# A four-layer graph network on one core: the small matmuls grouped into three visits a group, one pool of eight PSUM banks, and the first layer's coefficients planned one step earlier

## The chip, the cores and the metric

The kernel runs on one core of one Trainium2 chip. The metric is device time in microseconds (us) for one execution of the whole program. A core has five engines that take their instructions in order, each from its own stream: TensorE (PE in the profile; its weight loads are listed apart as PEld), VectorE (DVE), ScalarE (ACT), GpSimd (POOL) and SyncE (SP), which here issues the DMA transfers. TensorE writes its results to PSUM, which this kernel cuts into eight banks of 128 partitions by 512 floats.

## The reference, cut to what matters

The input is `x`, 128 graphs of 64 nodes with 512 features each (fp32), a 64 by 64 adjacency matrix for each graph, and a node mask of ones. Four layers follow each other, each inside a residual connection and a layer norm:

```python
# layer 0
s = (x @ w) @ a
A = tanh((s_i + s_j) / 8) * 8;  A = where(A >= 0, A, 0.1 * A)
A = exp(A) * adj;  A = A / A.sum(-1);  A = A * adj.sum(-1)
out0 = A @ x @ w
# layer 1
weight = adj * exp(q @ k.T);  out1 = (weight / weight.sum(-1)) @ v
# layer 2
agg = adj @ (k * mask);  w = mask * sum(q * agg, -1) / sqrt(512)
out2 = softmax(w over the nodes) * v
# layer 3 (hypergraph convolution, twice: 512 -> 1024 -> 512)
h = layer_norm(relu(Dn * (H @ (Be * (H.T @ (x @ W1)))) + b1))
out3 = Dn * (H @ (Be * (H.T @ (h @ W2)))) + b2 + x
# each layer
x = layer_norm(x + out)
```

`q`, `k` and `v` are products of `x` with 512 by 512 weights, and `H` is the pattern of the nonzero entries of `adj`.

## The kernel before, in words

**Tiling.** Two graphs make one tile of 128 tokens, two tiles make a group of 256 tokens, and there are 32 groups. The four layers of one group are written out in `run(g)` (line 962) as 16 steps. What depends on the adjacency alone is made for two groups at a time in `prepare_chunk` (line 656), so the work repeats with a period of two groups.

**How the order comes about.** Nothing is issued while `run(g)` is executed. Every instruction, or small bundle of instructions, is recorded as an `Op` (line 55) with its engine, an estimated cost, the buffers it reads and writes, and a key. The key of an operation of group g starts at `BASE[g]` plus its place among the 16 steps; the starts of neighbouring groups are 4 apart, so about four groups are under way at once, each in another layer. `keys_by_what_follows` (line 101) moves each key according to the length of the work that still depends on the operation, and keeps the lead that it was given (`urgent`). `Order.run` (line 118) then plays through a schedule: for each engine it keeps a heap of operations whose inputs are there, and takes the one with the lowest key for which all needed buffers are free. It then emits them in the order found, and the engine wrapper `pinned` (line 1127) fixes that order. All instructions pass through one line of this wrapper, so every row of the profile says L1133, and the rows are told apart by the names of the tiles they write and read.

**TensorE's forms.** The planner knows four modes of a PE operation. "whole" uses the 128 by 128 array at once. "quarters" divides it into four 64 by 64 arrays, and "columns" into two of 128 by 64. "any" can be done in either way: `over_graph` (line 926), which sums a column over the nodes of a graph, is one 128-row matmul in the whole array or two 64-row ones in quarters. The program counts in matmuls; the profile shows about two records for each (21227 for 10870).

- The large products with weights run whole. `seven_products` (line 806) does a block product with seven multiplications of half-size blocks in place of eight. Two running sums stay in a pair of PSUM banks (names `chx` and `chz` in the profile) and two more products take a single bank each (`bank`).
- `gathered` (line 764) multiplies tokens by a 64 by 64 matrix for each graph, as 16 small matmuls for each tile, in quarters. It is called four times for each group: once in layer 0 (`bank<-e,x`), once with `gm` in layer 3 on `x` and twice on the hidden `h` (`bank<-kept,h`). An ACT copy takes the result out of PSUM.
- `scores` (line 910) runs in columns, 8 matmuls for each tile (`bank<-k,k`), in layers 1 and 2.
- `emit_po` (line 1025) applies layer 1's weights to `v`: four matmuls of 512 columns in quarters (`bank<-k,e`).
- `emit_g` in `prepare_chunk` prepares the adjacency in quarters (`bank<-kept,kept`, `bank<-ones,adj`, `bank<-w,kept`).

A stretch of PE work between leaving the whole array and coming back to it is called a visit to the divided array below. In `Order.run`, a PE operation in the mode that the array is in may be preferred to one with a lower key, if its key is at most `NEAR` (0.5, while whole) or `FAR` (6.0, while divided) higher. A change of mode is charged with 145 or 60 ns (`TURN`, `TURN_DIVIDED`).

**PSUM.** Four banks are of the kind "bank", and two pairs of the kind "pair" take the other four (lines 284 to 286). If an operation cannot start because buffers are lacking, all kinds that it needs are put on hold for later operations of that engine in that search (`held.update(need)`).

**Layer 0's coefficients** are lines 971 to 993: for each tile a row product with `u0_b` on DVE and a scaled diagonal on ACT, then `over_graph` on PE, tanh on ACT, a DVE step, exp on ACT, a DVE product with the adjacency, `over_graph` again, a reciprocal and a last product on DVE. Then `gathered` of step 1 uses them.

**Transfers.** SP streams the weights from DRAM into eight buffers (`ring`, `streamed`, line 622). It may run ahead of the lowest unfinished step by `AHEAD` (3.5). The token tiles are loaded by `load_x` (line 359), whose key lies 6 ahead of the group's start.

Of the kernel before, what the change touches and what calls it, by code (L numbers as in the profile page):

```python
# [54 lines left out]
class Op:  # L55
    __slots__ = ("engine", "cost", "emit", "key", "missing", "users", "takes", "touches", "start", "bytes", "step", "mode", "port", "behind", "group", "args")


class Order:
# [4 lines left out]

    NEAR, FAR = 0.5, 6.0
    AHEAD = 3.5

    def __init__(self, slots):
        self.slots = {kind: list(range(n))[::-1] for kind, n in slots.items()}
        self.ops, self.key, self.group = [], 0.0, None  # L70

    def add(self, engine, cost, reads, writes, emit, urgent=0.0, size=0, mode=None, port=False):
        o = Op()
        o.engine, o.cost, o.emit, o.key, o.step = engine, cost, emit, self.key - urgent, self.key
        o.start, o.mode, o.port, o.behind, o.group, o.args = None, mode, port, None, self.group, ()
        o.users, o.takes, o.touches, o.bytes = [], [], [], size
        before, bufs = set(), []
        for tokens, write in ((reads, False), (writes, True)):
            for b in tokens:
                b, cells = b if isinstance(b, tuple) else (b, range(b.cells))  # L80
                if b not in bufs:
                    bufs.append(b)
                for c in cells:
                    if c in b.writer:
                        before.add(b.writer[c])
                    if write:
                        before.update(b.readers[c])
                        b.writer[c], b.readers[c] = o, []
                    else:
                        b.readers[c].append(o)  # L90
        before.discard(o)
        o.missing = len(before)
        for p in before:
            p.users.append(o)
        for b in bufs:
            b.left += 1
            if b.kind is not None:
                o.touches.append(b)
        self.ops.append(o)

    def keys_by_what_follows(self):
# [8 lines left out]
        for o in reversed(self.ops):  # L110
            if o.group is not None:
# [4 lines left out]
                o.key = o.step - urgent  # L116

    def run(self):

        ready = {e: [] for e in self.LATENCY}  # L120
        free_at = {e: 0 for e in self.LATENCY}
        number = {o: i for i, o in enumerate(self.ops)}
        events, n, link, mode = [], 0, 0, None
        port_free, port_user, landed = 0, None, []
# [5 lines left out]
        while len(done) < len(self.ops):  # L130
# [4 lines left out]
            for e, heap in ready.items():  # L135
                while free_at[e] <= now:
                    skipped, held, found = [], set(), None
                    while heap:
                        if e == "SP" and heap[0][0] > far or found and heap[0][0] > found[0] + (self.NEAR if mode == "whole" else self.FAR):
                            break  # L140
                        item = heappop(heap)
                        need = defaultdict(int)
                        wants = [b for b in item[2].touches if b.slot is None]
                        for b in wants:
                            need[b.kind] += 1
                        if item[2].port and port_free > now:
                            skipped.append(item)
                        elif all(k not in held and len(self.slots[k]) >= c for k, c in need.items()):
                            fits = e != "PE" or item[2].mode in (mode, "any")
                            if found is None or fits:  # L150
                                if found:
                                    skipped.append(found)
                                found, takes = item, wants
                            else:
                                skipped.append(item)
                            if fits or found[0] < 0:
                                break
                        else:
                            held.update(need)
                            skipped.append(item)  # L160
                    for item in skipped:
                        heappush(heap, item)
# [4 lines left out]
                    if e == "PE":  # L167
                        if found.mode == "any":
                            found.mode = "whole" if mode in ("whole", None) else "quarters"
                            found.args = (found.mode == "whole",)  # L170
                        if found.mode != mode:
                            turn = self.TURN if "whole" in (found.mode, mode) else self.TURN_DIVIDED
                        mode = found.mode
                    found.start = now
                    done.append(found)
# [59 lines left out]
def kernel(  # L235
# [47 lines left out]
    kind("col", 40, 16)  # L283
    kind("bank", 4, D, space=psum)
    pairs = [[psum.tile([P, D], FP, name=f"{c}{i}") for c in ("chx", "chz")] for i in range(2)]
    kinds["pair"] = pairs

# [7 lines left out]

    def pe(cost, reads, writes, emit, urgent=0.0, mode="whole"):
        order.add("PE", cost, reads, writes, emit, urgent, mode=mode)

    def dve(n, reads, writes, emit, urgent=0.0, port=None):

        if port is None:
            port = all((b[0] if isinstance(b, tuple) else b).kind not in ("bank", "pair") for b in reads)
        order.add("DVE", w_dve(n), reads, writes, emit, urgent, port=port)
# [352 lines left out]
    def prepare_chunk(c):  # L656
# [31 lines left out]

        pe(720, [turned, hA, bh, w], [*ps, gm], emit_g, mode="quarters")
        for t in range(2):  # L690
# [73 lines left out]
    def gathered(tokens, view, right, reads):  # L764
# [13 lines left out]
        for t in range(GT):  # L778
            pe(470, [tokens(t), *reads], [ps[0][t], ps[1][t]], lambda t=t: emit(t), mode="quarters")
        for h in range(2):  # L780
# [25 lines left out]
    def seven_products(a, s, pieces, first, more, across=False):  # L806


        pieces = iter(pieces)
        pair = Buf("pair", 2)  # L810

        def times(ps, left, start=True):
            piece, view = next(pieces)
            bank = (lambda: pair.t[ps]) if isinstance(ps, int) else (lambda: ps.t)
            token = pair[ps] if isinstance(ps, int) else ps
# [3 lines left out]
            def emit():  # L819
                l, b, o = left[1](), view(), bank()  # L820
                if across:
# [9 lines left out]

            pe(w_pe(P, 2 * chunks) if across else w_pe(width, chunks), [left[0], piece], [token], emit)
            return token, lambda: bank()[:, :width]

# [27 lines left out]
    def scaled_into(at, f, own, n, base=None):  # L862


        def add(k, token, ps, base):
            dst = at[k]
            t = own.start + int(k[0]) - 1
            dve(n + 40, [token, f, base[0]], [dst[0]], lambda: nc.vector.scalar_tensor_tensor(
                dst[1](), ps(), f.t[:, t : t + 1], base[1](), ALU.mult, ALU.add), NOW)
# [4 lines left out]
    def plain_into(b):  # L874

        at = block_views(b, lambda: b.t.rearrange("p (t d) -> p t d", t=GT))
        return (lambda k, token, ps: act(D // 2, [token], [at[k][0]], lambda: nc.scalar.copy(at[k][1](), ps()), NOW),
                lambda k, token, ps: dve(D // 2, [token, at[k][0]], [at[k][0]],
                                         lambda: nc.vector.tensor_add(at[k][1](), ps(), at[k][1]()), NOW))
# [30 lines left out]
    def scores(xT, zT):  # L910

        ps = Buf("bank", GT)
        for t in range(GT):
# [8 lines left out]

            pe(480, [xT[xT_cells(t)], zT[xT_cells(t)]], [ps[t]], emit, mode="columns")
        return ps

    def over_graph(v, ps):
# [5 lines left out]

        pe(w_pe(P), [v], [ps], emit, mode="any")

    def z_into(zT, bias=None):
# [11 lines left out]
        def first(k, token, ps):  # L947
            if bias is None:
                act(2 * P, [token], [cell(k)], lambda: nc.scalar.copy(at(k), two(ps)), NOW)
            else:  # L950
                for c in range(2):
                    col = 2 * (int(k[1]) - 1) + c
                    act(P + 100, [token, bias], [cell(k)], lambda c=c, col=col: nc.scalar.activation(
                        at(k)[:, c], two(ps)[:, c], AF.Identity, bias=bias.t[:, col : col + 1]), NOW)

        def more(k, token, ps):
            dve(2 * P, [token, cell(k)], [cell(k)], lambda: nc.vector.tensor_add(at(k), two(ps), at(k)), NOW)

# [3 lines left out]
    def run(g):  # L962
# [10 lines left out]


        s = Buf("col", GT)
        diag, e, ps_s = Buf("e", GT), Buf("e", GT), Buf("bank")
# [15 lines left out]
        dve(7 * GT * N, [ps_e], [rs], lambda: nc.vector.reciprocal(flat(rs.t), ps_e.t[:, : GT * N]), NOW)  # L992
        dve(GT * N, [e, rs], [e], lambda: nc.vector.tensor_mul(e.t, e.t, rs.t))
        step(1)
        left = left_side(gathered(*of_x, lambda h, t: e.t[halves[h][0], t, :], [e]))
# [34 lines left out]

        pe(w_pe(D), [e1, v], po, emit_po, mode="quarters")
        for t in range(GT):
# [171 lines left out]
```

## Time and profile before

The execution that was profiled is one of the four runs.

| | us |
|---|---|
| runs | 2172.2, 2174.02, 2174.33, 2179.66 |
| median | 2174.17 |
| the profiled execution, its own time | 2172.2 |
| its span, first to last instruction | 2170.3 |
| PE busy within the span | 2143.8 |
| DVE / ACT / POOL busy | 1534.9 / 854.6 / 384.2 |

The time of an execution is 1.9 us longer than the span. In a wait, the name behind the arrow is what released the engine; "issue" stands where the profile shows nothing that the engine waited for.

The stream of instructions itself is fetched by its own DMA queue (q8 in the table of queues), in 168 packets and 2.75 MB, that is 16 KB a packet. PE and PEld together have 42454 records, and 168 packets to those come to about 256 instructions a packet.

### The profile page before, as it was taken

How to read it: one execution, taken by the hardware profiler on the slowest of the kernel's cores; microseconds unless marked ns; L12 is line 12 of the kernel's file. 1: busy time of each engine (PE TensorE's matmuls, PEld its weight loads, DVE VectorE, ACT ScalarE, POOL GpSimd, SP SyncE). 2: the span in 40 equal slices, each digit the busy share in tenths (PEclk: the TensorE clock that was granted, in tenths of full speed). 3: DMA queues.
4: the chain of work that ended last, by engine and by line, in shares of the span. 5: the costliest groups of instructions: out<-in, count | busy, mean ns of one | idle time of the engine just before them, and what ended most of it. 6: DMA issues, size and time to landing. Idle time of an engine off the chain costs nothing.

```text
span 2170.3 us, 52324 instructions
## 1 busy us (share of the span) xinstructions
PE 2143.8 (99%) x21227; PEld 1727.3 (80%) x21227; DVE 1534.9 (71%) x3967; ACT 854.6 (39%) x1812; POOL 384.2 (18%) x399
## 2 busy tenths in 40 slices
PE   8999999999999999999999999999999999999998
PEld 4897787777888878888878888778888788888866
DVE  5787767677776767767676776767767777666675
ACT  2444343343443433443434443434434334333433
POOL 1112211021120212112122111211202221112111
PEclk9999999999999999999999999999999999999999
DMA  9865667656656666666576556666566666566476
GB/s 302 292 216 209 214 212 272 232 198 229 218 196 222 202 229 216 228 205 212 199 237 227 210 195 219 221 234 219 192 216 206 232 222 212 196 211 216 152 254 207
DMA packets 174304, 476.39 MB, mean 220 GB/s; under 512 B 35760, under 2 KB 45296, under 8 KB 174064
## 3 DMA queue, kind: packets, MB, share of 16 engines
q1 hardware_dynamic: 174064, 473.05, 64.0%
q8 instruction: 168, 2.75, 0.5%
q14 instruction: 72, 0.59, 0.1%
HBM read 443.33 MB, written 29.66 MB: 218 GB/s over the span
## 4 chain that ended last, share of the span: by engine, by line
PE 98%; DMA 1%; ACT 0%; issue 0%; DVE 0%; SPq 0%; DVEq 0%; ACTq 0%
PE bank L1133 40%; PE chx L1133 35%; PE chz L1133 23%; DMA ring<-w 0%; ACT k L1133 0%; DMA k<-in_wk_dram 0%; DMA ring<-3b 0%; ACT x L1133 0%; DVE col L1133 0%; DVE x L1133 0%; ACT u_b L1133 0%; ACT bw_b L1133 0%; SPq L1133 0%; DVEq L1133 0%; ACTq L1133 0%
## 5 line engine op out<-in xcount | busy, mean ns | idle before, releaser
L1133 PE MATMUL chx<-ring,k 128*128 128x256 f32 (+1 forms) x1664 | 477.2, 417 | 1.4 <-ACT k L1133 1.2
L1133 PE MATMUL bank<-ring,k 128*128 128x256 f32 (+1 forms) x1536 | 420.5, 416 | 0.3 <-ACT k L1133 0.3
L1133 PEld LDWEIGHTS chx<-ring,k 128*128 128x128 f32 x1664 | 309.0, 190 | 94.9 <-issue 56.2
L1133 POOL TENSOR_TENSOR col<-col,mhalf 128x2 f32<-128x2 f32 (+1 forms) x161 | 111.4, 692 | 1416.2 <-DVE col L1133 578.9
L1133 PEld LDWEIGHTS bank<-ring,k 128*128 128x128 f32 x1536 | 284.7, 190 | 82.9 <-issue 51.1
L1133 ACT COPY k<-bank 128x512 f32<-128x512 f32 (+1 forms) x448 | 228.1, 559 | 227.4 <-PE bank L1133 200.4
L1133 ACT ACTIVATE x<-x,col,col 128x512 f32<-128x512 f32 x256 | 195.4, 808 | 237.6 <-DVE col L1133 237.2
L1133 PE MATMUL chz<-ring,h 128*128 128x256 f32 (+1 forms) x768 | 242.8, 452 | 0.0
L1133 DVE SCALAR_TENSOR_TENSOR x<-chx,col,x 128x256 f32<-128x256 f32 x384 | 173.9, 478 | 73.0 <-PE chx L1133 70.8
L1133 PEld LDWEIGHTS chx<-k,m 128*128 128x128 f32 x1536 | 191.1, 192 | 26.1 <-issue 24.3
L1133 PE MATMUL chx<-k,m 128*128 128x128 f32 x1536 | 203.9, 276 | 0.0
L1133 PE MATMUL chz<-ring,k 128*128 128x256 f32 x768 | 200.4, 386 | 0.0
L1133 DVE SCALAR_TENSOR_TENSOR x<-bank,col,x 128x256 f32<-128x256 f32 (+1 forms) x256 | 137.5, 548 | 81.5 <-PE bank L1133 78.1
L1133 PEld LDWEIGHTS chz<-ring,h 128*128 128x128 f32 x768 | 142.6, 190 | 49.6 <-issue 34.9
L1133 PE MATMUL chx<-ring,h 128*128 128x256 f32 (+1 forms) x640 | 181.4, 422 | 0.1
L1133 DVE BATCH_NORM_STATS2 col<-x 128x6 f32<-128x512 f32 x256 | 174.8, 688 | 7.2
L1133 PEld LDWEIGHTS chz<-ring,k 128*128 128x128 f32 x768 | 140.8, 191 | 21.4 <-issue 2.4
L1133 PEld LDWEIGHTS chx<-ring,h 128*128 128x128 f32 x640 | 120.4, 190 | 35.3 <-issue 18.9
L1133 DVE SCALAR_TENSOR_TENSOR x<-chz,col,x 128x256 f32<-128x256 f32 x192 | 92.3, 481 | 76.4 <-PE chz L1133 75.8
L1133 PEld LDWEIGHTS chz<-k,m 128*128 128x128 f32 x1024 | 127.2, 192 | 12.8 <-issue 12.4
L1133 ACT ACTIVATE h<-h 128x512 f32<-128x512 f32 x128 | 80.7, 632 | 140.7 <-DVE h L1133 140.3
L1133 PE MATMUL chz<-k,m 128*128 128x128 f32 x1024 | 135.2, 275 | 0.0
(120 smaller groups left out, 2795.9 us busy)
## 6 DMA issues: line engine op xcount, KB each, us to landing
ring<-3a SPq DMA_DIRECT2D x224, 512.0 KB, 4.5
ring<-3b SPq DMA_DIRECT2D x224, 512.0 KB, 4.3
ring<-v SPq DMA_DIRECT2D x189, 512.0 KB, 4.4
ring<-w SPq DMA_DIRECT2D x93, 512.0 KB, 4.4
x<-in_x_dram SPq DMA_DIRECT2D x32, 512.0 KB, 4.9
ring<-v SPq DMA_DIRECT2D x63, 256.0 KB, 3.5
out_dram<-x SPq DMA_DIRECT2D x31, 512.0 KB, 4.6
ring<-w SPq DMA_DIRECT2D x31, 256.0 KB, 5.0
```

Source lines behind the costliest of these rows:

```text
L1133: made = f(*args, **kwargs)
```

## The change

Four things change.

1. **The choice of the next PE operation.** It moves to a function `choose`, which sees all operations that could start. While the array is whole, it turns to divided work only if that work's lowest key is below the lowest whole key by more than `NEAR` (now 0.8), or by more than 0 if at least `ENOUGH` (48) small matmuls are waiting. While it is divided, it goes on with divided work that is within `FAR` (now 4.0) of the lowest whole key, the same mode first, up to `BURST` (84) matmuls in one visit. Each divided operation now carries its number of matmuls. An operation of mode "any" is taken when it has the lowest key, in the mode the array is in.
2. **PSUM.** The two pairs and the four banks become one pool of eight banks. `seven_products` takes two of them as its pair, and a token of a new kind `product`, of which there are three, limits how many block products are under way.
3. **Holding back.** An operation that cannot start puts only those kinds on hold that it lacks.
4. **Layer 0's coefficients** get keys that are one step lower (`EARLY`), from the row product to the last product.

```diff
-    NEAR, FAR = 0.5, 6.0
+    NEAR, FAR = 0.8, 4.0
+    ENOUGH = 48
+    EARLY = 1.0
+    BURST = 84
     AHEAD = 3.5
...
-        o.engine, o.cost, o.emit, o.key, o.step = engine, cost, emit, self.key - urgent, self.key
+        o.engine, o.cost, o.emit, o.key, o.step = engine, cost, emit, self.key - urgent - self.early, self.key
...
+    def choose(self, found, mode, burst):
+
+        whole, either = found.get("whole", []), found.get("any", [])
+        divided = sorted(found.get("quarters", []) + found.get("columns", []), key=lambda f: f[0][:2])
+        first = min((f[0] for f in (whole, divided, either) if f), key=lambda f: f[0][:2])
+        if first[0][0] < 0 or first[0][2].mode == "any" or not (whole and divided):
+            return first
+        if mode == "whole":
+            ahead = whole[0][0][0] - divided[0][0][0]
+            enough = sum(f[0][2].matmuls for f in divided) >= self.ENOUGH
+            return divided[0] if ahead > (0 if enough else self.NEAR) else whole[0]
+        fits = [f for f in divided if burst + f[0][2].matmuls <= self.BURST and f[0][0] <= whole[0][0][0] + self.FAR]
+        if not fits:
+            return whole[0]
+        same = [f for f in fits if f[0][2].mode == mode]
+        return (same or fits)[0]
...
-                        if e == "SP" and heap[0][0] > far or found and heap[0][0] > found[0] + (self.NEAR if mode == "whole" else self.FAR):
+                        if e == "SP" and heap[0][0] > far:
                             break
...
-                            fits = e != "PE" or item[2].mode in (mode, "any")
-                            if found is None or fits:
-                                if found:
-                                    skipped.append(found)
+                            if e == "PE":
+                                skipped.append(item)
+                                found_pe.setdefault(item[2].mode, []).append((item, wants))
+                                if item[0] < 0:
+                                    break
+                            else:
                                 found, takes = item, wants
-                            else:
-                                skipped.append(item)
-                            if fits or found[0] < 0:
                                 break
                         else:
-                            held.update(need)
+                            held.update(k for k, c in need.items() if k in held or len(self.slots[k]) < c)
                             skipped.append(item)
+                    if found_pe:
+                        found, takes = self.choose(found_pe, mode, burst)
+                        skipped.remove(found)
...
+                        burst = 0 if mode == "whole" else burst + found.matmuls
...
-    kind("bank", 4, D, space=psum)
-    pairs = [[psum.tile([P, D], FP, name=f"{c}{i}") for c in ("chx", "chz")] for i in range(2)]
-    kinds["pair"] = pairs
+    kind("bank", 8, D, space=psum)
+    kinds["product"] = [None] * 3
...
-        pe(720, [turned, hA, bh, w], [*ps, gm], emit_g, mode="quarters")
+        pe(720, [turned, hA, bh, w], [*ps, gm], emit_g, mode="quarters", matmuls=40)
...
+        going, pair = Buf("product"), [Buf("bank") for _ in range(2)]
         pieces = iter(pieces)
-        pair = Buf("pair", 2)
...
-            pe(w_pe(P, 2 * chunks) if across else w_pe(width, chunks), [left[0], piece], [token], emit)
-            return token, lambda: bank()[:, :width]
+            pe(w_pe(P, 2 * chunks) if across else w_pe(width, chunks), [left[0], piece, going], [token], emit)
+            return (token, going), lambda: token.t[:, :width]
...
+        order.early = order.EARLY
         s = Buf("col", GT)
         diag, e, ps_s = Buf("e", GT), Buf("e", GT), Buf("bank")
...
         dve(GT * N, [e, rs], [e], lambda: nc.vector.tensor_mul(e.t, e.t, rs.t))
+        order.early = 0.0
         step(1)
```

`gathered` gets `matmuls=16`, `scores` 8, `over_graph` 2 and `emit_po` 4, and the readers of a product's result take its token pair. No instruction's arithmetic, shape or count on DVE, ACT, POOL or SP is edited; the number of PE matmuls depends on the mode in which the planner finds the array at each `over_graph`.

## The prediction

> **What bounds the kernel now.** I read the page's share of each engine first, then its chain of waits.
>
> ```profile
> span 2170.3 us, 52324 instructions
> PE 2143.8 (99%) x21227; PEld 1727.3 (80%) x21227; DVE 1534.9 (71%) x3967; ACT 854.6 (39%) x1812; POOL 384.2 (18%) x399
> PEclk9999999999999999999999999999999999999999
> PE 98%; DMA 1%; ACT 0%; issue 0%; DVE 0%; SPq 0%; DVEq 0%; ACTq 0%
> ```
>
> PE is busy for 99% of the span, at full clock in every slice, and it is 98% of the chain. So a gain can only come from fewer or cheaper turns inside PE's stream, or from the few waits that PE has. The PE waits of the whole run are the next view: what was waited for, total us, times, longest.
>
> ```profile
> PE bank L1133 <- issue: 6.4, 6, 3.4
> PE bank L1133 <- DMA k<-in_wk_dram: 6.1, 1, 6.1
> PE bank L1133 <- DVE e L1133: 3.4, 2, 2.2
> PE bank L1133 <- ACT k L1133: 1.5, 3, 0.7
> PE chx L1133 <- ACT k L1133: 1.2, 1, 1.2
> PE bank L1133 <- ACT u_b L1133: 0.7, 1, 0.7
> ```
>
> The wait for the first weights (6.1) is not touched. Of the others about 13 us are within reach. What a visit to the divided array costs is hidden in "busy"; the timeline of PE shows it (start, us, records):
>
> ```profile
> 1006.43 1.06 PE L1133 MATMUL chx<-k,m 128*128 128x128 f32 x8
> 1007.42 1.15 PE L1133 MATMUL bank<-k,k 128*64 128x64 f32 x32
> 1008.50 0.33 PE L1133 MATMUL bank<-e,same 64*64 64x128 f32 x2
> ...
> 1009.44 0.41 PE L1133 MATMUL bank<-e,same 64*64 64x128 f32 x4
> 1009.78 1.13 PE L1133 MATMUL chx<-ring,k 128*128 128x256 f32 x4
> 1010.75 1.05 PE L1133 MATMUL bank<-k,m 128*128 128x128 f32 x8
> ```
>
> I go by starts, since records overlap. Within a mode a 128x256 record takes 216 ns, a 128x128 one 112, a pair of 128x64 59, four 64x64 ones 58. From 1006.43 to 1007.42 eight records of 112 (0.90) take 0.99: +0.09 for the entry. The first divided bundle is +0.05 late, the last takes +0.09 longer, and the first whole product behind it takes 0.97 instead of 0.86: +0.10. Together a visit costs 0.335 us, and a turn from columns to quarters within it about 0.148.
>
> Two stretches of two groups each, the kernel's period (us; PE, PEld, DVE, ACT, POOL busy; clock, DMA share, GB/s), show a steady state in which PE has no gap except in one of them:
>
> ```profile
> 1007.42:1139.35 131.93, 131.67 (x1326) 106.96 (x1325) 93.54 (x245) 52.43 (x111) 23.18 (x24) 1.00 0.64 215
> 1139.35:1270.75 131.40, 131.40 (x1326) 106.84 (x1325) 93.55 (x245) 52.34 (x111) 23.17 (x24) 1.00 0.64 216
> ```
>
> **The change part by part.**
>
> *Turns.* Counted in the two programs' instruction order, the visits go from 118 to 107 (seven per two groups become six), and turns within a visit from 56 to 61. So 11 x 0.335 = -3.7 and 5 x 0.148 = +0.7. `over_graph` now mostly runs whole: 74 calls change from two 64-row matmuls (0.212 us) to one of 128 rows (0.223), +0.8. Sum **-2.2**. This is small next to the words "three visits a group": before already has 3.5.
>
> *Fetch of instructions.* The waits put down to "issue" are these (PE timeline, one place):
>
> ```profile
> 428.26 1.16 PE L1133 MATMUL bank<-e,x 64*64 64x64 f32 x64
> 429.24 0.87 PE L1133 MATMUL bank<-kept,h 64*64 64x64 f32 x44
> 433.49 0.51 PE L1133 MATMUL bank<-kept,h 64*64 64x64 f32 x18 [3.38 <-issue]
> ```
>
> PE stops in the middle of a bundle whose inputs it has. Counting PE and PEld records along the run, eight such stops (240, 341, 430, 766, 1029, 1293, 1556 and 1885 us) lie at the same place modulo 256, and the instruction queue has moved about 256 instructions a packet. So I read them as a fetched block that comes late. They cost 0.31, 0.87, 3.54, 0.44, 0.42, 0.18, 0.90 and 1.16, 7.8 us together with those too short for the waits view. From the passing of one boundary to the resumption behind the next, 2.5 to 3.7 us go by (once 5.7). Dense small matmuls use 256 instructions in 1.87 us (64 matmuls, each a weight load and a pass for two records, at 58 ns per four), so two gathers in a row outrun the fetch. Priced with the durations of before, before's order has 16 pairs of boundaries between 1.83 and 3.12 us, more than ten of them under 2.6; the shortest in the changed order are 2.68, 2.95, 2.96 and 3.00, because `emit_po`'s slow instructions (16 in 0.92 us) now lie between two gathers. If a block takes 3.0 us, 0.4 us of stops remain; at 3.7, 4.8. I take 1.6, so **-6.2** (ends -7.8 and -3.0; +2 if a 5.7 falls on a short pair, as at 430 us).
>
> The Trainium skill, "Runtime: NRT & Kernel Launch", section "Instruction fetch mechanics", says that crossing a 16 KiB boundary of 256 instructions is mostly hidden, since instructions go out slower than blocks come in. By it this term would be 0 and the sum 2168.0 us. The 6.4 us of "issue" waits and their regular spacing speak against it here, so the measurement decides.
>
> *PSUM pool.* At 498.65 us a gather waits 0.90 us for a bank until ACT has copied it out, the largest part of the 1.5 in the row "bank <- ACT k"; the other places are 0.1 to 0.35. One pool of eight removes what came from the split into four and two pairs. **-1.0** (ends -1.5 and +0.5, if the pair of a product now has to wait for banks that gathers hold).
>
> *Coefficients a step ahead.* In the steady state they cost nothing before: no PE wait for `e` appears behind 60 us. A step is about 16.4 us (131.4 for 8 keys). Moved are six DVE, five ACT and two PE bundles a group; no DMA, nothing on SP or POOL. They need the token tile, which is loaded 6 steps ahead and lands in a median of 4.9 us, so 5 steps are cover enough. DVE (71%) and ACT (39%) keep their work, only earlier. The gain is at the start:
>
> ```profile
> 50.75 0.49 PE L1133 MATMUL bank<-e,same 128*128 128x128 f32 x2 [1.16 <-DVE e L1133]
> 53.45 1.99 PE L1133 MATMUL bank<-e,x 64*64 64x64 f32 x64 [2.22 <-DVE e L1133]
> 56.60 2.08 PE L1133 MATMUL chx<-ring,k 128*128 128x256 f32 x4 [1.16 <-ACT k L1133]
> ```
>
> Three waits, 4.5 us, and behind the idle time the clock is low: the gather takes 1.99 where the one at 428.26 takes 1.16, and eight product records take 3.4 instead of 1.7, together another 2.5. In the changed order three products (0.86 each) and `emit_g` (0.8) stand between the second `over_graph` and the gather, where before has none; against that DVE works some 3.7 us between the reciprocal and the last product. Some 1.5 to 2.1 of the first two waits remain, the 1.16 for ACT's copy remains, half of the slow clock goes. **-3.0** (ends +1.0, if DVE's row is late by more than the products cover, and -5.8).
>
> *What the larger visit adds.* This is the one new dependence. A visit of 84 matmuls is 16 of `scores`, 32 of a gather, `emit_po`, 32 of a gather. `emit_po` needs those scores through an ACT exp (0.28 us) and a DVE product (0.29); before it lay one visit later, 3.3 us or more behind. Now only the 32 gather matmuls (0.93 us) lie between, and with the latencies between engines some 0.29 us are left at 24 places. Behind it in PE's queue stand 32 matmuls and the next product, so what is late here is late for all. ACT and DVE take their instructions in order: a copy of 128x512 (559 ns on ACT) or a BN_STATS (688 on DVE) in front of the two uses up the margin. Ends: 0, and 24 x 0.70 = +16.8 (one such instruction in front each time). Before had 14 places of `over_graph` and some 50 of product pairs with margins of 0.2 to 0.3 and no wait at them, which is the nearest row, so I take 24 x 0.08 = **+2.0**.
>
> Sum: -2.2 - 6.2 - 1.0 - 3.0 + 2.0 = -10.4, and 2172.2 - 10.4 = 2161.8. The median of the runs stands 2.0 above the profiled execution. Fetch stops, which need not repeat, are part of that, so I carry half of it over: **2163**, or 11 below the median. A measurement tells about 0.3% (6.5 us) from no change, so 2167.6 is the bound of "faster".
>
> **The rivals.**
>
> *The forecast holds in kind (0.70):* 2155 to 2168 from the ends of the fetch, start and turn terms.
>
> *`emit_po` waits a little in each large visit (0.12).* For it: the margin of 0.29. Against: places as tight passed freely before. 24 x 0.45 = +10.8 in place of +2.0 gives 2172, the same.
>
> *`emit_po` waits for a normalization (0.09), the other side.* If ACT's exp is queued behind a normalizing ACTIVATE (808 ns) and DVE's product behind a BN_STATS (688), each of the 24 visits loses about 1.2 us, and the 32 matmuls behind it too: +28.8 in place of +2.0 gives 2190. It decides the sign from (11 + 2)/24 = 0.5 us a visit, and makes it measurably slower from 0.8. For it: DVE is busy for 71% of the time. Against: ACT is idle for 61%, and both long instructions would have to stand in front in the same visit.
>
> *The fetch stops only move (0.06).* Blocks are consumed at the same mean rate, and a stop of 3.4 came where the others had 0.2 to 0.9, so chance may fill the gap: 7.8 us stay, 2169, the same.
>
> *The change hardly does what it says (0.03).* Only the 11 visits go, start and fetch stay: 2.2 below the median, 2172.
>
> **How the numbers follow.** The forecast's own range is 2155 to 2168, and of its 0.70 some 0.66 lies below 2167.6; low ends of the other three small cases add 0.06: faster 0.73. The same takes 0.18 (the rest of the forecast, the small wait, the moved stops, the turns alone). Slower, over 2180.7, is the normalization rival, 0.09. Up to 2172 the range holds the forecast and part of the same: 2154 to 2172.
>
> **What the profile of the changed kernel would show.** Six visits to the divided array per two groups, and stretches of about 131.1 us in place of 131.40 where nothing stops; "issue" waits of PE at 2 us or less instead of 6.4; the two waits for `e` before 60 us at about 2 instead of 3.4; no wait of a gather for ACT's copy in the middle. The prediction is wrong if PE rows `bank<-k,e` carry a wait for DVE `e` in group after group, if "issue" stays near 6, or if PE begins to wait for `ring` transfers (DMA share 64%, no such wait now).

## The result, and the profile after

The changed kernel takes 2180.05 us (median of 43 runs, 2170.76 to 2193.22), the kernel before 2174.14 (63 runs, 2169.62 to 2180.11). The ratio is 1.0027, with a 95% interval of 1.002 to 1.0035. So it is slower by some 6 us, just inside the 0.3% that the prediction called "same", where 11 us of gain were forecast. It also scatters over 22 us instead of 10. The execution that was profiled took 2177.19 us, 5.0 more than the one of before.

The page of the changed kernel, and the PE waits of the whole run (total us, times, longest):

```profile
span 2175.3 us, 51970 instructions
PE 2144.3 (99%) x21079; PEld 1730.9 (80%) x21079; DVE 1531.9 (70%) x3967; ACT 852.7 (39%) x1812; POOL 384.3 (18%) x399
PE 98%; issue 1%; DVE 0%; DMA 0%; ACT 0%; SPq 0%; DVEq 0%; ACTq 0%
```

```profile
PE bank L1156 <- issue: 13.7, 10, 2.0
PE bank L1156 <- DMA k<-in_wk_dram: 6.2, 1, 6.2
PE bank L1156 <- DVE e L1156: 1.9, 1, 1.9
PE bank L1156 <- ACT k L1156: 1.2, 1, 1.2
PE bank L1156 <- ACT u_b L1156: 0.7, 1, 0.7
PE bank L1156 <- ACT x L1156: 0.2, 1, 0.2
```

"issue" has gone up from 6.4 us to 13.7; no other wait grew by more than 0.2. The waits for `e` and for banks shrank, and no `emit_po` waits for `e`, which had been the prediction's fear. What a large visit looks like, first undisturbed (its window of PE's timeline at 684 us), then at 946 us:

```profile
684.08 1.15 PE L1156 MATMUL bank<-k,k 128*64 128x64 f32 x32
685.16 1.16 PE L1156 MATMUL bank<-kept,h 64*64 64x64 f32 x64
686.14 1.04 PE L1156 MATMUL bank<-k,e 64*64 64x512 f32 x8
687.00 1.11 PE L1156 MATMUL bank<-kept,h 64*64 64x64 f32 x64
688.04 2.21 PE L1156 MATMUL bank<-ring,k 128*128 128x256 f32 x9
```

```profile
946.30 1.15 PE L1156 MATMUL bank<-k,k 128*64 128x64 f32 x32
947.38 1.16 PE L1156 MATMUL bank<-kept,h 64*64 64x64 f32 x64
948.36 1.04 PE L1156 MATMUL bank<-k,e 64*64 64x512 f32 x8
949.22 0.88 PE L1156 MATMUL bank<-kept,h 64*64 64x64 f32 x48
952.05 0.46 PE L1156 MATMUL bank<-kept,h 64*64 64x64 f32 x16 [1.96 <-issue]
952.45 5.41 PE L1156 MATMUL bank<-ring,k 128*128 128x256 f32 x16
```

Undisturbed, the 84 matmuls take 3.96 us. At 949.9 us PE stops for 2 us in the middle of a gather. Behind the stop 16 product records take 5.41 us, where 16 at 216 ns take 3.5. Two stretches show that as well (us; PE, PEld, DVE, ACT, POOL busy; clock, DMA share, GB/s):

```profile
731.49:862.60 131.11, 131.11 (x1319) 106.85 (x1313) 93.79 (x245) 52.35 (x111) 23.19 (x24) 1.00 0.64 217
953.01:956.42 3.41, 3.41 (x10) 2.70 (x9) 1.57 (x3) 0.60 (x2) 0.00 (x0) 0.50 0.03 10
```

The first is a period of two groups in which nothing stops: 131.11 us, 0.29 less than before, as forecast. The second is a stretch at half the clock, 3.41 us long, that loses 1.7 us. The changed kernel has three of these in mid-run (953.0, 1287.5, 2154.5), the kernel before has none; both have one of 6.83 us behind the start and one at the end. The page's clock row cannot show this, since a 9 there means 90% or more of a slice of 54 us; the prediction's "at full clock in every slice" claimed more than that row says.

How the two profiled executions differ along the run follows from the amount of matmul work done (each record at its in-mode cost): the changed kernel is 2 us ahead after the start, 9.7 ahead at 800 us of work, 5.3 at 1000, even at 1800, and 4.8 behind at the end. So a gain is made where nothing stops, and it is given back at the stops and the slow stretches behind them.

The stops follow a strict rule in both traces. Matching each 16 KB packet of the instruction queue with PE's stream (matmuls, weight loads and semaphore instructions, 42826 records in the trace of the changed kernel): all ten long stops of the changed kernel and all eight of before end 1.3 to 1.5 us after a packet has landed, and all lie at one place modulo 256, some 64 instructions ahead of a multiple of it. The packet takes 0.96 us (median). What differs is when it starts. Such a place, one in every 256 instructions, is called a boundary here: PE stops at one until the block is there whose fetch started after PE had passed the boundary before. In the changed kernel's stops it starts 1.7 to 3.8 us after PE passed the boundary before; in those of before 0.1 to 1.3, but for one of 3.3.

### The profile page after: what moved, and what is told of

Its sections match the earlier page's. It is cut to its first block, busy times and chain, and to the rows that moved or that the text cites. A ratio compares the mean times of both kernels' runs of the same rounds, so it can differ in the third digit from the quotient of the medians.

```text
span 2175.3 us, 51970 instructions
## 1 busy us (share of the span) xinstructions
PE 2144.3 (99%) x21079; PEld 1730.9 (80%) x21079; DVE 1531.9 (70%) x3967; ACT 852.7 (39%) x1812; POOL 384.3 (18%) x399
## 4 chain that ended last, share of the span: by engine, by line
PE 98%; issue 1%; DVE 0%; DMA 0%; ACT 0%; SPq 0%; DVEq 0%; ACTq 0%
PE bank L1156 98%; DMA k<-in_wk_dram 0%; DVE col L1156 0%; ACT x L1156 0%; DVE x L1156 0%; ACT k L1156 0%; ACT u_b L1156 0%; SPq L1156 0%; DVE e L1156 0%; DVEq L1156 0%; ACTq L1156 0%
## 5 line engine op out<-in xcount | busy, mean ns | idle before, releaser
L1156 PE MATMUL bank<-ring,k 128*128 128x256 f32 (+1 forms) x3968 | 1040.4, 412 | 5.5 <-issue 4.3
L1156 PEld LDWEIGHTS bank<-ring,k 128*128 128x128 f32 x3968 | 738.5, 192 | 195.5 <-issue 95.4
L1156 DVE SCALAR_TENSOR_TENSOR x<-bank,col,x 128x256 f32<-128x256 f32 (+1 forms) x832 | 400.1, 500 | 228.1 <-PE bank L1156 218.8
L1156 PEld LDWEIGHTS bank<-k,m 128*128 128x128 f32 x3584 | 429.9, 192 | 23.8 <-issue 10.4
L1156 PE MATMUL bank<-k,m 128*128 128x128 f32 x3584 | 437.1, 276 | 0.0
L1156 PE MATMUL bank<-ring,h 128*128 128x256 f32 (+1 forms) x1408 | 418.4, 440 | 0.0
L1156 PEld LDWEIGHTS bank<-ring,h 128*128 128x128 f32 x1408 | 257.7, 190 | 85.4 <-issue 60.4
L1156 DVE TENSOR_TENSOR k<-bank,k 128x256 f32<-128x256 f32 x384 | 154.1, 421 | 149.3 <-PE bank L1156 147.4
L1156 DVE TENSOR_TENSOR k<-k 128x256 f32<-128x256 f32 x226 | 103.7, 459 | 32.7 <-ACT k L1156 30.9
L1156 PE MATMUL bank<-k,k 128*64 128x64 f32 (+1 forms) x2112 | 105.4, 238 | 6.9 <-DMA k<-in_wk_dram 6.2
```

The source lines that it names most:

```text
L1156: made = f(*args, **kwargs)
```

## The experiments

Theory A: PE stops because a block of 256 instructions comes late, and late because its fetch waits behind weight transfers that are in flight. Theory C: the dense visits alone outrun the fetch. Theory F: the fetch has nothing to do with the time. The first four runs:

**The weight loads cut to a sixteenth**, in each kernel:

```diff
-out=t_.t[:, : n * width], in_=src.t[:, : n * width]
+out=t_.t[:8, : n * width], in_=src.t[:8, : n * width]
```

> The changed kernel, but each streamed weight load brings 8 of its 128 partitions (a sixteenth of the bytes), with the same number of loads in the same order; the rest of a weight buffer keeps what an earlier load left there, so the products are not the reference's. Theory A (PE stops because a block of 256 instructions comes late, and it comes late because its fetch waits behind weight transfers in flight): the fetch starts 0.3 to 1 us after PE passes a boundary instead of 1.7 to 3.8, PE's issue waits fall from 13.7 us to 3 or less, the half-clock stretches behind them go, and the time is 2156 to 2163. Theory C (the dense visits alone outrun the fetch, whatever the other transfers do): issue waits stay at 10 to 15 us and the time at 2175 to 2182. Theory F (the fetch has nothing to do with it): the time stays within 3 us of the changed kernel's 2180.

> The same cut of the weight loads to 8 of 128 partitions in the kernel before. Theory A: little is lost there to transfers in flight (its stops had fetches that started 0.1 to 1.3 us after the boundary, but for one of 3.3): issue waits go from 6.4 to 2 to 5 us, the time to 2165 to 2171. Theory C: issue waits stay near 6 and the time near 2174.

The changed kernel took 2157.12 us (4 runs, 2156.97 to 2158.63), 0.9924 of before (0.9911 to 0.9937); the cut kernel before 2165.51 (4 runs, 2163.76 to 2166.48). "issue" in the cut changed kernel, then in the cut kernel before:

```profile
PE bank L1156 <- issue: 0.3, 1, 0.3
```

```profile
PE bank L1133 <- issue: 1.9, 2, 1.7
```

With the visits as dense as ever, the stops are gone, the half-clock stretches in mid-run too, and the runs lie within 2 us. C and F fall. For boundaries that PE passes while the array is divided, the fetch starts 0.7 us later in the median, against 2.2 in the changed kernel; the cut kernel before has 0.7 against 1.1. The difference 2157.1 - 2165.5 = -8.4 is what the change brings where the fetch is quick. In the profiled executions 1.6 of it is "issue", and some 1.7 more is the half-clock stretch behind the start, 10.24 us long in the cut kernel before and 6.83 in the other.

**Smaller visits**, and **the coefficients at their old place**:

```diff
-    BURST = 84
+    BURST = 52
```

```diff
-    EARLY = 1.0
+    EARLY = 0.0
```

> The changed kernel with BURST 52 in place of 84: 148 visits to the divided array instead of 107, none with more than 208 matmul and load instructions. Theories A and C: no 256 instructions go out within 4 us, so issue waits fall to 1 us or less and the half-clock stretches in mid-run go (-15 and -5 us); 41 visits more cost 41 x 0.335 = 13.7; time about 2170, and the runs spread as little as before's. Theory F (visits and their order cost, not the fetch): 2180 + 13.7 = 2194.

> The changed kernel with EARLY 0, layer 0's coefficients at their old keys: 129 visits to the divided array instead of 107, still 24 of 84 matmuls. Theory A: 22 visits more cost 7.4 us, the start loses the 2 us that it had gained, the stops stay as they are because the large visits stay: 2185 to 2192, with the same wide spread. Rival (the early coefficients hold buffers or engines and cost time in the steady state): 2172 to 2178.

With 52 the time is 2181.91 us (5 runs, 2181.09 to 2185.5; 1.004, 1.0028 to 1.0052). The fetch did what theory A said, "issue" is down to 0.4 us, but the 2170 were missed, for a wait that I had not costed. The PE waits behind 60 us:

```profile
PE bank L1156 <- ACT k L1156: 7.4, 10, 0.9
PE bank L1156 <- issue: 0.4, 2, 0.3
```

The second gather of `h` now stands in a later visit, and the product behind it waits for ACT's copy of it. With the turns: 2157.1 + 13.7 + 7.4 = 2178.2; 3.7 us stay unexplained.

With EARLY 0 it is 2186.92 us (6 runs, 2182.84 to 2189.98; 1.0058, 1.0045 to 1.0072), as expected: the large visits and their stops (10.2 us of "issue") stay, and the early coefficients are what had saved 22 visits.

**Transfers held back at every visit.** An experiment that leaves all bytes in place: transfers that the plan starts from 1.5 us before a visit until its end wait for the visit's last matmul. PE's order is untouched.

```diff
+    HOLD = 1500
...
+    def hold(self, done):
...
+                    visits.append((first.start - self.HOLD, final))
...
+            if o.engine == "SP" and visit and o.start >= visit[0]:
+                o.behind = visit[1]
+                held.append(o)
+                continue
...
-    for o in order.run():
+    for o in order.hold(order.run()):
...
+        elif o.engine == "PE":
+            names[o] = last[str(mybir.EngineType.PE)]
```

> The changed kernel with PE's order untouched; every transfer that the plan starts between 1.5 us before a visit to the divided array and the visit's end is made to wait for the visit's last matmul. All loads keep their bytes. Theory A (fetches of instructions wait behind weight transfers in flight): fetches in the visits start within about 1 us of the boundary, issue waits fall from 13.7 to 5 us or less, mid-run half-clock stretches mostly go, time 2158 to 2168. If instead the weights now come late, PE shows waits for ring transfers and the time is above 2175. Theory C (density alone): issue waits stay above 10 us.

> The same holding back of transfers in the kernel before. Theory A: its 6.4 us of issue waits fall to 2 to 5 us, the time to 2166 to 2172. If the weights come late, PE waits for ring transfers and the time is above 2178.

The changed kernel went to 2171.52 us (12 runs, 2166.22 to 2182.22; 0.9981, 0.9968 to 0.9994), over the 2158 to 2168 of theory A, and the kernel before to 2191.14 (4 runs, 2189.83 to 2191.39; 1.0065, 1.005 to 1.008). The PE waits, of the changed kernel held back and of the kernel before held back:

```profile
PE bank L1187 <- issue: 5.0, 5, 2.5
PE bank L1187 <- DVE h L1187: 4.3, 2, 2.2
```

```profile
PE bank L1164 <- ACT k L1164: 9.8, 12, 2.1
...
PE bank L1164 <- issue: 4.8, 6, 1.8
PE chx L1164 <- ACT k L1164: 4.7, 3, 3.3
```

The stops inside the visits shrank (the one at 950 us from 2.1 to 0.8 us), but two fetches started 4.7 and 5.6 us late, and new waits appeared. The put-off loads do not explain these two: ahead of both boundaries the loads lay as in the changed kernel, whose fetches there came within 1 us. Three half-clock stretches in mid-run stayed, which theory A had mostly gone: one behind a stop of 2.5 us for instructions, two behind waits of 2.1 and 2.2 us for `h`. The kernel before lost 15 us against its own time in the same rounds (2176.34) where I had expected a gain. Only 0.6 us of its PE waits are for a `ring` transfer, so most of the loss came by way of other engines, and I did not follow it further.

**One part undone: PSUM split as before.**

```diff
-    kind("bank", 8, D, space=psum)
-    kinds["product"] = [None] * 3
+    kind("bank", 4, D, space=psum)
+    pairs = [[psum.tile([P, D], FP, name=f"{c}{i}") for c in ("chx", "chz")] for i in range(2)]
+    kinds["pair"] = pairs
...
```

> The changed kernel with the old PSUM split (four banks and two pairs, no limit of three products); choice of the next PE operation, holding back and early coefficients stay. The plan comes out with 130 visits of at most 64 matmuls but for three of 80. Theory A: no dense visit, so issue waits of 2 us or less and a narrow spread; 23 visits more than the changed kernel cost 7.7 us on the 2157 that it takes without stops: 2163 to 2172. If the pool itself is what costs time in the changed kernel, it is also below 2172 but the issue waits stay near 13.

It took 2178.54 us (11 runs, 2175.78 to 2183.38; 1.0011, 1.0002 to 1.0019): the narrow visits brought few stops, but again gathers stand alone, and products and banks wait for ACT's copies.

```profile
PE bank L1158 <- ACT k L1158: 7.4, 11, 0.7
...
PE bank L1158 <- issue: 3.3, 2, 2.0
```

So the pool of eight, with its limit of three products, is what lets both gathers of `h` into one visit; without it the choice rule pays 23 more visits and 7.4 us of waits. The 2163 to 2172 were missed mostly for the same wait as with 52: 2157.1 + 7.7 + 7.4 + 3.3 = 2175.5, and 3.0 us stay unexplained.

**Fewer instructions for the same work.** Each gather's matmuls of 64 by 64 that share rows become one of 64 rows by 128 columns:

```diff
-                    for f, (cols, _) in enumerate(halves):
-                        at = (c * GT + t) * N
-                        nc.tensor.matmul(ps[h].t[cols, at : at + N], view(t)[rows, c * P + f * N : c * P + f * N + N],
-                                         right(h, t), start=True, stop=True)
+                    at = (c * GT + t) * N
+                    nc.tensor.matmul(ps[h].t[:, at : at + N], view(t)[rows, ts(c, P)],
+                                     right(h, t), start=True, stop=True)
```

> The changed kernel, same order, but each pair of 64x64 matmuls of a gather that share the rows is one matmul of 64 rows by 128 columns: 2048 instead of 4096 small matmuls, 208 instead of 336 matmul and load instructions in a large visit. Theories A and C: issue waits of 1 us or less and no half-clock stretch in mid-run. What a 64x128 matmul costs no trace shows: as much as the two that it replaces (29 ns a record) gives 2157; twice that (58 ns) adds 4096 x 29 ns = 119, 2276. The nearest row is the 128x64 one of 29.5, so I expect 2157 to 2170.

It took 2274.45 us (4 runs, 2271.43 to 2275.24; 1.0447). There is no "issue" wait at all, but 32 records take 2.00 us where 64 of the small ones, which do the same work, took 1.16:

```profile
715.01 2.00 PE L1155 MATMUL bank<-kept,h 64*128 64x64 f32 x32
```

That is the upper end of what I had expected, 58 ns a record: 2157.1 + 4096 x 29 ns = 2275.9. My choice of the nearest row was wrong.

**Holding back only where two boundaries fall close together, and a control.** The trace of the changed kernel had named the visits at risk, so the held set was cut to 15 of the 106 visits of the plan (a 64-row transposition at the start made the prediction's 107), and in the control to 15 others:

```diff
+    HOLD = 2000
+    HELD = [21, 30, 35, 38, 41, 50, 53, 62, 65, 68, 72, 80, 83, 92, 105]
...
+        held, visits = [], iter([v for i, v in enumerate(visits) if i in self.HELD])
```

```diff
+    HOLD = 2000
+    HELD = [26, 29, 32, 44, 47, 56, 59, 71, 74, 77, 86, 89, 95, 23, 98]
```

> The changed kernel, PE's order untouched, transfers held back (from 2 us before a visit to its end) at 15 of the 106 visits only: those during which PE passes two boundaries of 256 instructions within 5.6 us. Theory A: the stops inside these visits (949, 1019, 1616, 1682, 1882, 2152 us and those just behind them) shrink to 0.8 us or less each, without the bunching of loads that holding at every visit made: issue waits 2 to 5 us instead of 13.7, at most one half-clock stretch in mid-run, time 2160 to 2168. Rival (holding helps by spreading the transfers, wherever it is done): no better than holding at other visits.

> The control to the run before: transfers held back in the same way at 15 other visits, 13 of them of 84 matmuls, in which PE passes at most one boundary within 5.6 us. Theory A: nothing is gained, issue waits of 10 to 16 us at the same places as in the changed kernel, time 2176 to 2186. Rival (it is the spreading of the transfers): as fast as the run before, 2160 to 2168.

Held at the visits at risk: 2161.41 us (5 runs, 2159.56 to 2165.37), 0.994 of before (0.9927 to 0.9952), the fastest of all kernels that do the whole work, 13 us under before and 19 under the changed kernel. The control: 2177.98 (12 runs, 2170.03 to 2181.15; 1.0001, 0.9988 to 1.0013). The same visit as above in the first of them (PE and SP timelines), then in the control:

```profile
947.96 1.16 PE L1188 MATMUL bank<-kept,h 64*64 64x64 f32 x64
948.94 1.04 PE L1188 MATMUL bank<-k,e 64*64 64x512 f32 x8
949.80 1.16 PE L1188 MATMUL bank<-kept,h 64*64 64x64 f32 x64
950.89 2.86 PE L1188 MATMUL bank<-ring,k 128*128 128x256 f32 x12
```

```profile
951.04 0.32 SPq L1188 DMA_DIRECT2D ring<-w  x1
951.45 1.68 SPq L1188 DMA_DIRECT2D ring<-3b  x2
```

```profile
953.30 1.04 PE L1188 MATMUL bank<-k,e 64*64 64x512 f32 x8
954.16 0.88 PE L1188 MATMUL bank<-kept,h 64*64 64x64 f32 x48
956.30 0.46 PE L1188 MATMUL bank<-kept,h 64*64 64x64 f32 x16 [1.26 <-issue]
```

And the "issue" rows of both:

```profile
PE bank L1188 <- issue: 2.2, 1, 2.2
```

```profile
PE bank L1188 <- issue: 15.1, 11, 2.7
```

In the changed kernel loads were issued at 944.7, 945.5 and 946.4, just ahead of the visit or at its start; here they go out at 951, behind it, the fetch starts 0.3 us after the boundary instead of 2.7, and PE runs through. Eight of the control's eleven stops are in the same visits as those of the changed kernel. The control is 0.6% slower than the run that it controls, so where the loads are held matters. But it is not quite without a gain: its ratio of 1.0001 lies under the 1.0027 of the changed kernel, some 6 us, and the two intervals do not touch. So part of the 19 us may come from spreading the loads, as the rival has it; the control's profile, with 15.1 us of "issue", does not show where.

**The held set made shorter, and the same care for the kernel before** (the diff is that of the runs above with other numbers of visits: the ten that remain of the 15, and 15 of the kernel before):

> As the run that held transfers back at 15 visits, but without the five in which the second boundary comes 4.9 us or more after the first; its only long issue wait (2.2 us at 508 us) lay beside one of those, with a fetch that started 5.4 us late behind loads that had been put off. Theory A: that wait goes, the short windows stay covered, issue waits of 0 to 3 us: 2157 to 2163. If the five mattered, stops come back there (335, 625 us): 2160 to 2166.

> The kernel before, its PE order untouched, with transfers held back at the 15 visits after the start in which PE passes two boundaries within 3.3 us. Theory A: issue waits fall from 6.4 to 2 us or less, its own stops (7.8 us) mostly go: 2166 to 2170. The distance to the changed kernel with the same care, some 8 us, is then what the change brings by its turns, waits and start. If holding costs here as it did at all visits (waits for ACT copies): 2175 or more.

Ten visits give 2163.88 us (5 runs, 2158.24 to 2166.45; 0.9952, 0.9939 to 0.9965), within the scatter of fifteen. The stop at 508 us stayed (2.5 us of the 5.1 us of "issue"), against the expectation:

```profile
508.31 0.48 PE L1188 MATMUL bank<-ring,h 128*128 128x256 f32 x1
511.28 2.16 PE L1188 MATMUL bank<-ring,h 128*128 128x256 f32 x5 [2.49 <-issue]
```

Nothing is held in this run before 660 us, so loads that were put off did not make it; up to there the transfers and matmuls are those of the changed kernel, in the same order. Around this boundary both profiled executions issued the same seven loads at the same distances from it, and the fetch started 0.95 us behind it in the changed kernel and 5.8 here. So the same traffic gives a quick fetch in one execution and a stop in the next, and which stops a single profile shows is partly chance. Stops at 334 and 628 us came back, in windows of about 5 us, as the second reading had it; one at 1434 us, in a window of the same length, is not in the profile of the changed kernel.

The kernel before gains nothing: 2175.06 us (11 runs, 2173.02 to 2178.7; 1.0005, 0.9996 to 1.0014). Its "issue" fell from 6.4, and one gather came to wait for its tokens:

```profile
PE bank L1165 <- issue: 3.5, 5, 0.9
PE bank L1165 <- ACT x L1165: 3.4, 1, 3.4
```

I had expected 2166 to 2170. All but one of its stops had quick fetches already (0.1 to 1.3 us), so there was little for the hold to remove, and 3.4 us of new wait ate that.

## Why the prediction was wrong

*Fetch of instructions: the step that failed.* The working was "If a block takes 3.0 us, 0.4 us of stops remain; at 3.7, 4.8. I take 1.6, so -6.2". The mechanism is right, down to the place in the stream and the windows at risk: from one boundary to the next the cut changed kernel needs 2.9 us at the shortest, and eight of the ten stops lie in windows of some 3.7 us or less. The size and the sign are wrong, because 2.5 to 3.7 us was taken for a property of the fetch. It had been read off the stops of before, where all fetches but one started within 1.3 us. In the changed kernel's stops the block takes 4.0 to 6.3 us from boundary to resumption. Measured in the profiled executions: stops 15.3 us instead of 7.8, and 5.1 us at half clock instead of none, so +12.6 in place of -6.2.

That the loads in flight make these fetches late is shown by the cut loads and by the loads held back, with which the fetches at the same places mostly started within 1 us of the boundary. Their number is not what tells the two kernels apart, though. Of the boundaries that PE passes in the divided array, 77 of 84 have two or more transfers in flight (issued and not yet landed) in the changed kernel, and 76 of 101 in the kernel before (where the landing of a quarter of the transfers is counted from the updates of their semaphores); at seven of the eight stops of before there were three to six. One of them (SP, then the stop, then the stretch from the boundary to the landing of the packet, with DMA share and GB/s last), and below it the same for the stop of the changed kernel at 950 us:

```profile
760.71 1.18 SPq L1133 DMA_DIRECT2D ring<-w  x2
762.44 0.32 SPq L1133 DMA_DIRECT2D ring<-3a  x1
766.42 0.46 PE L1133 MATMUL bank<-kept,h 64*64 64x64 f32 x16 [0.28 <-issue]
763.66:765.01 1.35, 1.35 (x72) 1.28 (x72) 1.22 (x4) 0.28 (x1) 0.00 (x0) 1.00 1.03 334
```

```profile
944.67 0.32 SPq L1156 DMA_DIRECT2D ring<-w  x1
945.54 1.18 SPq L1156 DMA_DIRECT2D ring<-3b  x2
947.00:950.62 3.62, 3.10 (x136) 2.38 (x133) 1.15 (x3) 1.35 (x3) 0.00 (x0) 1.00 0.76 243
```

Both times three loads were issued in the 3 us ahead of the boundary, and the DMA engines were busier in the kernel before (1.03 against 0.76); yet the packet started 0.2 us after the boundary there and 2.7 in the changed kernel. Why as many loads delayed the fetches of before so little stays open. The trace of before had a warning all the same: over all its fetches, not only those at stops, one in ten started 3.0 us or more after the boundary, which makes 5.4 us with the 0.96 of the packet and the 1.4 behind it. The 5.7 us at 430 us was one of these, and I had set it aside as chance. The rule that had been weighed against the rows, that crossing a block's boundary is mostly hidden (the Trainium skill, "Runtime: NRT & Kernel Launch", "Instruction fetch mechanics"), agrees with the run with the loads cut (0.3 us of "issue"), and not with the changed kernel (13.7).

*Turns, -2.2.* 0.29 us a period of two groups, as forecast (131.11). What the other terms leave of the 5.0 us is -4.2, so the term was rather too small; 0.29 in each of 16 periods would be 4.6.

*PSUM pool, -1.0.* The 0.90 at 498 us is gone; the two rows of waits for ACT's `k` went from 2.7 to 1.2, so -1.5. That the pool also makes the large visits possible, I had not seen.

*Coefficients, -3.0.* The waits for `e` at the start fell from 3.4 to 1.9, the one for ACT's copy stayed at 1.2, and the half clock behind them stayed at 6.83 us; it had been forecast to go by half. The changed kernel is 1.9 us ahead there. Nothing was lost in the steady state, and without the early keys there are 22 visits more.

*The larger visit, +2.0.* No `emit_po` waits: 0. Both rivals on it fall.

*The rivals.* "The fetch stops only move" (0.06) named the right mechanism and stopped too early: it held the rate and the latency fixed. The case that came, stops that grow, had no chance of its own; the text only gave it "+2" as an end.

Without the fetch the sum was -4.2, and the two cut kernels differ by 8.4, of which 1.6 is "issue" and some 1.7 the slow clock at the start.

## What to carry to other kernels

Dense small matmuls are an instruction rate, not only a PE time: 256 instructions in 3 us went through without a stop where the block behind them came in 3 us, and in the changed kernel that hung on the loads that were in flight just then. A latency that is read off the stalls in a trace is that of one kernel in one execution; take its spread over all transfers, and expect another execution to differ. A burst of small matmuls and the loads around it are worth planning together: with the loads put behind 15 of the visits, and PE's order untouched, the changed kernel became 19 us faster.

## What the runs showed of the hardware that was not expected

- Every long stop of PE in the two kernels ended 1.3 to 1.5 us after its block of instructions had landed, at one place modulo 256 in PE's stream. In the divided array the changed kernel's fetches started, in the median, 0.86 us after the boundary with at most one transfer in flight (7 fetches), 2.18 with two (27) and 2.69 with more (50); those of before 0.64 (25), 1.46 (28) and 1.58 (48). So the number in flight is not the whole of it, and at one boundary the same loads gave 0.95 us in one execution and 5.8 in another; which part of the queue a fetch waits behind stays open.
- A stop can cost twice: half-clock stretches of 3.41 us followed stops of 2.1 to 2.4 us at 950, 1285 and 2152 us, but not one of 2.15 at 1683, nor the 3.6 of before at 430. Waits of 2.1 and 2.2 us for `h`, in the changed kernel with loads held back at every visit, were followed by the same 3.41 us, so a wait for data does it too. What decides is open. In the 43 runs of the changed kernel the time goes with the mean clock (0.991 to 0.997, correlation -0.87).
- A matmul of 64 rows by 128 columns on 64 columns of data costs about 58 ns a record (117 us more for 2048 matmuls), twice the two quarter ones that it replaces.
